# A two-stage Strassen kernel on one Trainium2 core: the low-rank products of two units in one block, a second unit's products brought forward, and another order at the hand-over between the stages

## The chip, the cores and the metric

The kernel runs on one core of one Trainium2 chip. The metric is the device time of one execution in microseconds (us). Everything is in float32. The engines are named as in the profile: PE (TensorE, matmuls), PEld (its weight loads), DVE (VectorE), ACT (ScalarE), POOL (GpSimd) and SP (SyncE, which here only issues DMAs).

## What is computed

`x` is (32, 128, 2048): 32 sequences of 128 tokens. Two layers follow each other, each with a residual:

```python
# layer 0: a dense layer with bias, and a low-rank part chosen by adapter_id (one per sequence)
base  = einsum('bsi,oi->bso', x, weight) + bias          # weight (2048, 2048)
low   = einsum('bsi,bri->bsr', x, lora_a[adapter_id])    # rank 16
delta = einsum('bsr,bor->bso', low, lora_b[adapter_id])
x = x + base + scale[adapter_id] * delta
# layer 1: each sequence has its own (2048, 2048) weight, chosen by another id
x = x + einsum('bij,bkj->bik', x, weight1[adapter_ids])
```

## The kernel before

**Stage 1 (layer 0).** The dense product is made by the Strassen-Winograd scheme on two levels: 7 products in place of 8, at the price of sums and differences of the operands. The outer level is the list `PHASES`: 7 phases, each with the signed quadrants of x and of the weight that are added up to its operands, the partial sum that it reads (`old`), the one that it writes to DRAM (`new`: P1, U2, U3, U4), and, from phase 3 on, the output quadrant that it finishes (`final`). A phase has 8 units (2 groups `g` of sequences x 4 blocks `o` of 256 output channels), so there are 56 units, numbered `n`. Phases 3 to 6 are units 24 to 55.

The inner level is inside a unit: seven calls of `product(k, bank, n, start)`, four accumulating matmuls each (the profile counts two instructions for one float32 matmul), weights 128x128 stationary, 512 columns of x moving. They go in the order 1, 2, 6, 5, 7, 3, 4 into three PSUM banks: a takes products 1, 6, 7, 4, b takes 2, c takes 5 and 3. The sums accumulate in bank a, and ACT copies it out between them (p1 after product 1, u2 after product 6, u3 after product 7, the last quarter of z after product 4); it copies c after product 5. So product 6 adds onto bank a after ACT has copied p1 out of it. Banks a, b and c are double: even and odd units use different ones. DVE adds the banks and copies to the four quarters of `z` (buffer slot 19 or 20, by parity).

DVE also makes the inner operands: `w_sums(n)` (four sums of 128x512, the last three weight operands of `product` come from them), `w_terms` and `a_terms` (the outer sums of 128x2048), and `a_sums` once per four units. `finish(n)`, called at the head of unit n + 1, adds the partial sums and the residual x to z and stores z: to DRAM as a partial sum, or to `x1t`, the input of stage 2.

**The low-rank part.** In phase 1, `lowrank` (L444) makes `low` = scale x (x A), with a row of ones for the bias; `lowrank_out` scales it. `add_low(n, which)` (L491) multiplies it with B and the bias: for each of four 128-column pieces `s` and each of four 32-row groups `q` of the array, one matmul of 32 rows by 128 columns. Phase 3 ("apart", where the unit also has a partial sum to store and so z must stay free of it) sends two groups at a time to the banks d and l and adds them to the residual x. Phases 4 to 6 ("late") send all four at the end of the unit onto b, c, a and d. `load_b` gathers B for the next unit with eight small DMAs on POOL.

**Buffers and queues.** `mem` has 21 slots of 1 MB. `Loads` hands them out in one fixed order of loads: pool "A" (8 slots), "W" (3) and "st" (5, for outer terms, residual x and partial sums). A load is issued on SP when its slot is released, and a load that must wait for a slot holds up all behind it. Each engine runs its own instructions in program order.

**Stage 2 (layer 1).** Sixteen pairs of sequences, 8 steps each, one level of the same scheme: 56 instructions of 128x512 per step (L682), two sequences side by side in 64 columns each. `sums_w1(n)` (L216) adds the identity for the residual to the weight's diagonal blocks and makes the weight sums, all but one, which the function that it returns makes later (`fourth`). `sums_x1` (L248) makes the sums of x1; `load_w1` and `load_x1` load 4 MB and 1 MB. At the end of unit 55 `second_loads` and `second_sums` start this stage: they reuse slots of stage 1, among them slot 19 (z of unit 54) for the x1 sums. The last step has its own order and stores each output quarter as soon as it is ready.

Of the kernel before, what the change touches and what calls it, by code (L numbers as in the profile page):

```python
# [72 lines left out]
def cond_resid_kernel(  # L73
# [103 lines left out]
    def add(dst, a, b):  # L177
        nc.vector.tensor_tensor(dst, a, b, ALU.add)  # L178
# [83 lines left out]
    with tc.tile_pool(name="c0", bufs=1) as c0, tc.tile_pool(  # L262
# [12 lines left out]


        loads = Loads(
            {"A": range(8), "W": (13, 11, 12), "st": (17, 15, 16, 14, 18)}
        )

        def view(slot, *shape):
# [40 lines left out]
                    ),  # L322
                )

        def add_end(n):
            i, g, o = units[n]
            _, _, old, new, final = PHASES[i]

            def load_x(slot):
                r, c, _ = final  # L330
                for t in range(2):
                    nc.sync.dma_start(
                        out=view(slot, 2, 2, NF)[:, t],
                        in_=xq[r, g, t, c, o // 2, :, ts(o % 2, 2)],
                    )

            if final:
                loads.add(("x", n), "st", load_x)
            for k in (old, final[2] if final else None):
                if k:  # L340
                    loads.add(
                        (k, n), "st",
                        lambda slot, k=k: nc.sync.dma_start(out=mem[:, slot], in_=part[k, g, o]),
                    )
# [8 lines left out]
                    )  # L353

        add_w(0)
        for q in range(4):
            add_a(0, q)
        add_w(1)
        for n in range(len(units)):
            if n // 4 + 1 < 2 * len(PHASES):  # L360
                add_a(n // 4 + 1, n % 4)
            if n + 2 < len(units):
                add_w(n + 2)
            add_end(n)
# [123 lines left out]
                    start=(start and i == 0), stop=(i == 3), skip_group_check=True,  # L488
                )

        def add_low(n, which):  # L491

            i, g, o = units[n]
            r = PHASES[i][4][0]
            for s in range(4):
                for q, dst, start in which:
                    nc.tensor.matmul(  # L497
                        dst[:, ts(s, S)], lhsT=b_sels[n][ts(q, RT), s], rhs=low[r, g][ts(q, RT), s],
                        start=start, stop=True, skip_group_check=True,
                    )  # L500

        def zq(z, t, j):

            return z.rearrange("p (t s j m) -> p t s j m", t=2, s=4, j=2)[:, t, :, j]

        def by_seq(psum_bank):
            return psum_bank.rearrange("p (s m) -> p s m", s=4)

        def finish(n):

            i, g, o = units[n]
            _, _, old, new, final = PHASES[i]
            z = mem[:, 19 + n % 2]
            if new:
                w = z
                if old:
                    prev = mem[:, loads.slot((old, n))]
                    w = prev if final else z
                    add(w, prev, z)
                nc.gpsimd.dma_start(out=part[new, g, o], in_=w)  # L520
                if old:
                    loads.done((old, n))
            if final:
                r, c, k = final
                xs = view(loads.slot(("x", n)), 2, 2, 4, S)
                for t in range(2):
                    dst = z.rearrange("p (t s j m) -> p t j s m", t=2, s=4, j=2)[:, t]
                    add(dst, dst, xs[:, t])
                loads.done(("x", n))
                add(z, z, mem[:, loads.slot((k, n))])  # L530
                loads.done((k, n))
                for t in range(2):
                    nc.gpsimd.dma_start(  # L533
                        out=x1t[4 * r + 2 * g + t][:, :, 8 * c + 2 * o : 8 * c + 2 * o + 2].rearrange(
                            "s p j m -> p s (j m)"
                        ),
                        in_=view(19 + n % 2, 2, 4, 2 * S)[:, t],
                    )

        def second_loads():  # L540
            assert n == len(units) - 1 and 19 + n % 2 == 20
# [5 lines left out]
            load_x1(0, 0)  # L547
            load_w1(1)

        def second_sums(step):  # L550
            if step == 5:
                sums_x1(0, 0)
                state["fourth"] = sums_w1(0)
            else:
                state["fourth"]()

        state = {}
        acts, wts, b_sels = {}, {}, {}
        w_terms(0)
        wts[0] = w_sums(0)  # L560
        for _ in a_sums(0):
            pass
        w_terms(1)

        for n, (i, g, o) in enumerate(units):
            _, _, old, new, final = PHASES[i]
            a, b, c = (x[n % 2] for x in (bank_a, bank_b, bank_c))
            z = mem[:, 19 + n % 2]
            group = n // 4
            more = group + 1 < 2 * len(PHASES)  # L570
            lowering = more and (group + 1) // 2 == LOW
            apart = bool(new and final)
            late = final and not apart
            p1, u2, p5, u3 = (
                evp.tile([P, NF], F32, tag=k, name=k) for k in ("p1", "u2", "p5", "u3")
            )
            if n + 1 < len(units) and PHASES[units[n + 1][0]][4]:
                b_sels[n + 1] = load_b(n + 1)
            if n:
                finish(n - 1)  # L580
            if n == 2:
                make_scale()
            if n == len(units) - 2:
                load_w1(0)
            if n + 1 < len(units):
                wts[n + 1] = w_sums(n + 1)
            else:
                second_loads()
            sums = a_sums(group + 1) if more and o == 3 else iter(())

            product(1, a, n, True)
            nc.scalar.copy(p1, a)
            product(2, b, n, True)
            if lowering:
                lowrank(group + 1, o)
                loads.done(("a", group + 1, o))
            if more:
                a_terms(group + 1, o)
            if n + 2 < len(units):
                w_terms(n + 2)  # L600
            if lowering and o % 2 == 1:
                lowrank_out(group + 1, o // 2)
            if not late:
                add(zq(z, 0, 0), by_seq(b), by_seq(p1))
            product(6, a, n, False)
            nc.scalar.copy(u2, a)  # L606
            next(sums, None)
            product(5, c, n, True)
            nc.scalar.copy(p5, c)
            if n + 1 == len(units):  # L610
                second_sums(5)
            next(sums, None)
            if apart:
                add_low(n, [(0, bank_d, True), (1, bank_l, True)])
            product(7, a, n, False)
            nc.scalar.copy(u3, a)  # L616
            if apart:
                xs = view(loads.slot(("x", n)), 2, 2, NF)
                add(xs[:, 0, 0], bank_d, xs[:, 0, 0])
                add(xs[:, 0, 1], bank_l, xs[:, 0, 1])  # L620
            add(zq(z, 1, 1), by_seq(u3), by_seq(p5))
            next(sums, None)
            product(3, c, n, False)
            if apart:
                add_low(n, [(2, bank_d, True), (3, bank_l, True)])
            if not late:
                add(zq(z, 0, 1), by_seq(c), by_seq(u2))
            product(4, a, n, False)
            if apart:
                add(xs[:, 1, 0], bank_d, xs[:, 1, 0])  # L630
                add(xs[:, 1, 1], bank_l, xs[:, 1, 1])
            next(sums, None)
            if late:
                add_low(n, [(0, b, False), (1, c, False), (2, a, False), (3, bank_d, True)])
                add(zq(z, 0, 0), by_seq(b), by_seq(p1))
                add(zq(z, 0, 1), by_seq(c), by_seq(u2))
                add(zq(z, 1, 1), by_seq(bank_d), zq(z, 1, 1))
            nc.scalar.copy(zq(z, 1, 0), by_seq(a))  # L638
            loads.done(("W", n, 0))
            if o == 3:  # L640
                for q in range(4):
                    loads.done(("A", group, q, 0))
            if n + 1 == len(units):
                second_sums(4)
        finish(len(units) - 1)


    with tc.tile_pool(name="c1", bufs=1) as c1:
# [6 lines left out]
        for n in range(last + 1):  # L655
# [13 lines left out]
            elif n % 8 == 6 and pair + 1 < len(pairs):  # L669
                sums_x1(pair + 1, 0)  # L670

            def store(engine, h, c):

                cols = out.rearrange("b t (c m n) -> b t c m n", c=2, m=2)[:, ts(h, M), :, n2]
                for j, b in enumerate(pairs[pair]):
                    engine.dma_start(out=cols[b][:, c], in_=res[ts(j, M), h, c])

            for k in (1, 6, 7, 5, 2, 3, 4) if n == last else (1, 7, 2, 3, 5, 6, 4):
                dst = bank[:, banks[k]]
# [9 lines left out]
                if n == last:  # L689
# [98 lines left out]
```

## Time and profile before

| | us |
|---|---|
| median of 3 runs (lowest, highest) | 2994.54 (2992.4, 2995.85) |
| the profiled execution | 2994.32 |
| its span in the profile | 2992.7 |
| PE busy | 2976.9 |
| DVE busy | 2337.7 |
| ACT busy | 184.2 |
| POOL busy | 239.8 |

The span runs from the first to the last recorded instruction or transfer, and the profiled execution's own time is 1.6 us longer. A line of a group reads: source line, engine, operation, output<-input, shapes, count | busy us, mean ns | idle us of the engine before them and what ended it. Lines of the chain read: start us, length us, what. Stage 1 ends and stage 2 begins near 1443 us.

### The profile page before, as it was taken

The page shows a single profiled execution, that of the slowest core. Times are in us where ns is not written, and L with a number is a line of the kernel's source. Part 1 is how long each engine was busy: PE and PEld are TensorE (multiplying, and loading weights), DVE is VectorE, ACT ScalarE, POOL GpSimd, SP SyncE. Part 2 cuts the span into 40 slices and gives each one's busy share as a digit, 9 for nine tenths or more (in the row PEclk, how much of TensorE's full clock was granted, in tenths as well). Part 3 has the DMA queues.
Part 4 walks back from the last instruction along what each step waited for, and adds up shares of the span by engine and source line. Part 5 has one row for each costly group of instructions (what it writes and reads, how often), then busy time and mean ns, then how long its engine had stood idle before and what let it go on. Part 6 is the DMA issues. An engine that isn't in the chain of part 4 may idle for free.

```text
span 2992.7 us, 32904 instructions
## 1 busy us (share of the span) xinstructions
PE 2976.9 (99%) x12384; PEld 1178.5 (39%) x12384; DVE 2337.7 (78%) x1690; ACT 184.2 (6%) x313; POOL 239.8 (8%) x427
## 2 busy tenths in 40 slices
PE   9999999999999999999999999999999999999999
PEld 4445444444444444444333333333333333333333
DVE  3367755467655669773899999999999999999997
ACT  1111111111111111111000000000000000000000
POOL 1111000012222222221000000000000000000000
PEclk9999999999999999999999999999999999999999
DMA  5679966789866889985999999999999999999996
GB/s 225 239 307 360 343 255 253 266 316 353 311 246 225 305 341 392 393 311 207 367 394 390 390 387 404 388 395 390 402 390 394 393 385 404 385 398 385 407 387 226
DMA packets 186015, 1025.61 MB, mean 343 GB/s; under 512 B 23809, under 2 KB 23809, under 8 KB 79617
## 3 DMA queue, kind: packets, MB, share of 16 engines
q1 hardware_dynamic: 142432, 906.55, 76.5%
q0 software_dynamic: 25248, 83.92, 7.4%
q10 hardware_dynamic: 18176, 33.04, 3.5%
q8 instruction: 98, 1.61, 0.2%
q14 instruction: 61, 0.49, 0.0%
HBM read 922.76 MB, written 100.66 MB: 342 GB/s over the span
## 4 chain that ended last, share of the span: by engine, by line
PE 98%; DMA 1%; DVE 1%; SPq 0%; issue 0%; DVEq 0%
PE bank L682 51%; PE bank L486 44%; PE bank L497 1%; PE bank L453 1%; DMA mem<-in_w1q_dram 1%; DMA mem<-in_xq_dram 0%; DVE mem L181 0%; DVE mem L178 0%; SPq L211 0%; SPq L320 0%; SPq L303 0%; SPq L298 0%; DVE res L178 0%; SPq L243 0%; DVEq L178 0%
## 5 line engine op out<-in xcount | busy, mean ns | idle before, releaser
L181 DVE TENSOR_TENSOR mem<-mem 128x2048 f32<-128x2048 f32 (+1 forms) x733 | 1482.9, 2052 | 30.4 <-PE bank L486 6.3
L682 PE MATMUL bank<-mem 128*64 128x512 f32 x5120 | 1122.6, 593 | 4.4 <-DVE mem L181 2.4
L486 PE MATMUL bank<-mem 128*128 128x512 f32 x1792 | 792.5, 595 | 3.4 <-DMA mem<-in_xq_dram 3.4
L682 PEld LDWEIGHTS bank<-mem 128*64 128x64 f32 x5120 | 367.6, 137 | 737.0 <-issue 689.5
L486 PE MATMUL bank<-mem,tset 128*128 128x512 f32 x1344 | 597.6, 594 | 1.7 <-DVE mem L181 1.5
L486 PEld LDWEIGHTS bank<-mem 128*128 128x128 f32 x1792 | 338.3, 190 | 421.6 <-issue 417.1
L682 PE MATMUL bank<-mem,s 128*64 128x512 f32 x2048 | 461.2, 592 | 0.0
L178 DVE TENSOR_TENSOR mem<-mem 128x2048 f32<-128x2048 f32 (+2 forms) x193 | 338.7, 1769 | 124.9 <-ACT mem L638 56.9
L486 PEld LDWEIGHTS bank<-mem,tset 128*128 128x128 f32 x1344 | 253.7, 190 | 319.7 <-issue 315.7
L682 PEld LDWEIGHTS bank<-mem,s 128*64 128x64 f32 x2048 | 147.1, 137 | 292.4 <-issue 292.1
L178 DVE TENSOR_TENSOR mem<-u,p 128x512 f32<-128x512 f32 x56 | 38.7, 690 | 208.4 <-ACT u L616 208.4
L478 POOL DMA_DIRECT2D b_sel<-in_bt_dram x256 | 135.2, 528 | 580.7 <-PE bank L497 473.3
L178 DVE TENSOR_TENSOR mem<-bank,p 128x512 f32<-128x512 f32 x56 | 38.5, 687 | 126.1 <-PE bank L497 109.4
L688 ACT COPY pv<-bank 128x512 f32<-128x512 f32 x32 | 18.8, 586 | 1515.7 <-PE bank L682 1088.3
L178 DVE TENSOR_TENSOR pv<-bank,pv 128x512 f32<-128x512 f32 x64 | 44.3, 692 | 75.0 <-PE bank L682 74.0
L181 DVE TENSOR_TENSOR tset<-mem,tset 128x512 f32<-128x512 f32 x112 | 77.1, 689 | 8.9 <-PE bank L486 4.1
L178 DVE TENSOR_TENSOR mem<-mem,ident 128x1024 f32<-128x1024 f32 x64 | 78.0, 1219 | 0.0
L178 DVE TENSOR_TENSOR mem<-bank,u 128x512 f32<-128x512 f32 x56 | 38.4, 686 | 45.6 <-PE bank L486 45.6
L606 ACT COPY u<-bank 128x512 f32<-128x512 f32 x56 | 32.8, 586 | 391.8 <-PE bank L486 391.8
L638 ACT COPY mem<-bank 128x512 f32<-128x512 f32 x56 | 32.8, 586 | 387.0 <-PE bank L486 203.3
L533 POOL DMA_DIRECT2D x1t<-mem x64 | 49.2, 773 | 84.0 <-DVE mem L178 79.2
L497 PEld LDWEIGHTS bank<-low,b_sel 32*128 32x128 f32 x1024 | 39.1, 186 | 30.3 <-issue 27.3
(38 smaller groups left out, 519.2 us busy)
## 6 DMA issues: line engine op xcount, KB each, us to landing
mem<-in_w1q_dram SPq DMA_DIRECT2D x512, 1024.0 KB, 10.2
mem<-in_xq_dram SPq DMA_DIRECT2D x119, 1024.0 KB, 12.6
mem<-in_w0q_dram SPq DMA_DIRECT2D x111, 1024.0 KB, 6.9
mem<-U SPq DMA_DIRECT2D x40, 1024.0 KB, 9.0
mem<-in_xq_dram SPq DMA_DIRECT2D x66, 512.0 KB, 7.2
x1t<-mem POOLq DMA_DIRECT2D x64, 512.0 KB, 8.0
mem<-x1t SPq DMA_DIRECT2D x64, 512.0 KB, 9.1
out_dram<-res ACTq DMA_DIRECT2D x124, 256.0 KB, 6.0
```

The lines of the kernel that those rows point to most:

```text
L178: nc.vector.tensor_tensor(dst, a, b, ALU.add)
L181: nc.vector.tensor_tensor(dst, a, b, ALU.subtract)
L453: nc.tensor.matmul(banks_r[r][ts(s, RT), :S], lhsT=a_sel[:, r, s, 4 * k + i, :], rhs=piece[:, i, s, :], start=(h == 0 and seen[r] == 0 and ...
L478: nc.gpsimd.dma_start(out=b_sel[ts(t, 2 * RT), s], in_=bt[ds(m, 1), c, o].rearrange("o j r m -> (o j r) m"),)
L486: nc.tensor.matmul(dst, lhsT=wts[n][k][:, i, :], rhs=acts[n // 4][k][:, i, :], start=(start and i == 0), stop=(i == 3), skip_group_check=True,
L497: nc.tensor.matmul(dst[:, ts(s, S)], lhsT=b_sels[n][ts(q, RT), s], rhs=low[r, g][ts(q, RT), s], start=start, stop=True, skip_group_check=True,
L533: nc.gpsimd.dma_start(out=x1t[4 * r + 2 * g + t][:, :, 8 * c + 2 * o : 8 * c + 2 * o + 2].rearrange("s p j m -> p s (j m)"), in_=view(19 + ...
L606: nc.scalar.copy(u2, a)
L638: nc.scalar.copy(zq(z, 1, 0), by_seq(a))
L682: nc.tensor.matmul(dst[ts(j, M)], lhsT=xts[pair, k4 // 2][k][:, j, k4 % 2 * 2 + i], rhs=w1s[n][k][:, j, i], start=(k4 == 0 and i == 0), st ...
L688: nc.scalar.copy(pv[:, 0], dst)
```

## The change

In phase 3, `add_low(n)` runs once, at the head of the unit, for all four row groups, into the banks b, c, d and l, and DVE adds all four to x (`low_to_x`) there. In phases 4 to 6, an even unit ends with its own `add_low` and directly behind it that of the odd unit n + 1; for the odd one group 0 stays in its bank b (product 2 then adds to it, and now comes ahead of product 1) and the other three are added to its x. x of such a unit is loaded one unit earlier (`early`, `add_x`), and two slots of the pool "st" are swapped. At the start, the weights of unit 1 are loaded ahead of the last two quarters of x, its sums are made ahead of the activation sums, and its products 1 and 2 come between products 2 and 6 of unit 0. The last unit adds x to the partial sum first (`rest`), adds that to z by quarters, makes the first w1 sums ahead of the z addition behind product 7, and stores each half of z as it is ready, without `finish(55)`. The last output store uses SP's queue for one of its two DMAs.

```diff
-            {"A": range(8), "W": (13, 11, 12), "st": (17, 15, 16, 14, 18)}
+            {"A": range(8), "W": (13, 11, 12), "st": (17, 16, 15, 14, 18)}
...
+        def early(n):
+            return n < len(units) and PHASES[units[n][0]][4] and (
+                PHASES[units[n][0]][3] or n % 2 == 1
+            )
...
-            if final:
-                loads.add(("x", n), "st", load_x)
+            if early(n + 1):
+                add_x(n + 1)
+            if final and not early(n):
+                add_x(n)
...
-        for q in range(4):
+        for q in range(2):
             add_a(0, q)
         add_w(1)
+        for q in range(2, 4):
+            add_a(0, q)
...
-        def add_low(n, which):
+        def add_low(n, dsts, starts):
             for s in range(4):
-                for q, dst, start in which:
+                for q, (dst, start) in enumerate(zip(dsts, starts)):
                     nc.tensor.matmul(
                         dst[:, ts(s, S)], lhsT=b_sels[n][ts(q, RT), s], rhs=low[r, g][ts(q, RT), s],
-                        start=start, stop=True, skip_group_check=True,
+                        start=(start and s == 0), stop=(s == 3), skip_group_check=True,
                     )
+        def low_to_x(n, q, src):
+            xs = view(loads.slot(("x", n)), 4, NF)[:, q]
+            add(xs, src, xs)
...
         wts[0] = w_sums(0)
+        w_terms(1)
+        wts[1] = w_sums(1)
         for _ in a_sums(0):
             pass
-        w_terms(1)
...
-            late = final and not apart
+            late = final and not early(n)
+            ahead = early(n) and not apart
...
+            if apart:
+                low_banks = b, c, bank_d, bank_l
+                add_low(n, low_banks, (True,) * 4)
+                for q in range(4):
+                    low_to_x(n, q, low_banks[q])
             if n:
                 finish(n - 1)
...
-            product(1, a, n, True)
-            nc.scalar.copy(p1, a)
-            product(2, b, n, True)
+            if ahead:
+                product(2, b, n, False)
+            if n != 1:
+                product(1, a, n, True)
+                nc.scalar.copy(p1, a)
+                if not ahead:
+                    product(2, b, n, True)
+            if n == 0:
+                p1_next = c0.tile([P, NF], F32, tag="p1_next", name="p1_next")
+                product(1, bank_a[1], 1, True)
+                nc.scalar.copy(p1_next, bank_a[1])
+                product(2, bank_b[1], 1, True)
...
+            if ends:
+                rest = mem[:, loads.slot(("U4", n))]
+                for t in range(2):
+                    dst = rest.rearrange("p (t s j m) -> p t j s m", t=2, s=4, j=2)[:, t]
+                    add(dst, dst, view(loads.slot(("x", n)), 2, 2, 4, S)[:, t])
+                loads.done(("x", n))
             if not late:
                 add(zq(z, 0, 0), by_seq(b), by_seq(p1))
+            if ends:
+                add(zq(z, 0, 0), zq(z, 0, 0), zq(rest, 0, 0))
             product(6, a, n, False)
...
-            if n + 1 == len(units):
-                second_sums(5)
+            if ends:
+                fourth = sums_w1(0)
...
             add(zq(z, 1, 1), by_seq(u3), by_seq(p5))
+            if ends:
+                add(zq(z, 1, 1), zq(z, 1, 1), zq(rest, 1, 1))
+                sums_x1(0, 0)
...
             if not late:
                 add(zq(z, 0, 1), by_seq(c), by_seq(u2))
+            if ends:
+                add(zq(z, 0, 1), zq(z, 0, 1), zq(rest, 0, 1))
+                store_x1(n, 0)
             product(4, a, n, False)
...
             if late:
-                add_low(n, [(0, b, False), (1, c, False), (2, a, False), (3, bank_d, True)])
+                add_low(n, (b, c, a, bank_d), (False, False, False, True))
+                b1, c1, a1 = (x[1 - n % 2] for x in (bank_b, bank_c, bank_a))
+                add_low(n + 1, (b1, c1, a1, bank_l), (True,) * 4)
+                low_to_x(n + 1, 2, a1)
                 add(zq(z, 0, 0), by_seq(b), by_seq(p1))
                 add(zq(z, 0, 1), by_seq(c), by_seq(u2))
                 add(zq(z, 1, 1), by_seq(bank_d), zq(z, 1, 1))
-            nc.scalar.copy(zq(z, 1, 0), by_seq(a))
+                low_to_x(n + 1, 1, c1)
+                low_to_x(n + 1, 3, bank_l)
+            if ends:
+                add(zq(z, 1, 0), by_seq(a), zq(rest, 1, 0))
+                store_x1(n, 1)
+                loads.done(("U4", n))
+                fourth()
+            else:
+                nc.scalar.copy(zq(z, 1, 0), by_seq(a))
...
-            if n + 1 == len(units):
-                second_sums(4)
-        finish(len(units) - 1)
...
-                        store(nc.scalar, 1, 0)
+                        store(nc.scalar, 1, 0, nc.sync)
```

More of the change, by code (lines that the diff above doesn't have):

```diff
@@ L323, in add_a, with add_x @@
                 )
-        def add_end(n):
+        def early(n):
+            return n < len(units) and PHASES[units[n][0]][4] and (
+                PHASES[units[n][0]][3] or n % 2 == 1
+            )
+        def add_x(n):
             i, g, o = units[n]
-            _, _, old, new, final = PHASES[i]
             def load_x(slot):
-                r, c, _ = final
+                r, c, _ = PHASES[i][4]
                 for t in range(2):
@@ L335, in load_x, with add_end @@
                     )
-            if final:
-                loads.add(("x", n), "st", load_x)
+            loads.add(("x", n), "st", load_x)
+        def add_end(n):
+            i, g, o = units[n]
+            _, _, old, new, final = PHASES[i]
+            if early(n + 1):
+                add_x(n + 1)
+            if final and not early(n):
+                add_x(n)
             for k in (old, final[2] if final else None):
@@ L504, in zq, with store_x1 @@
             return z.rearrange("p (t s j m) -> p t s j m", t=2, s=4, j=2)[:, t, :, j]
+        def low_to_x(n, q, src):
+            xs = view(loads.slot(("x", n)), 4, NF)[:, q]
+            add(xs, src, xs)
         def by_seq(psum_bank):
             return psum_bank.rearrange("p (s m) -> p s m", s=4)
+        def store_x1(n, t):
+            i, g, o = units[n]
+            r, c, _ = PHASES[i][4]
+            nc.gpsimd.dma_start(
+                out=x1t[4 * r + 2 * g + t][:, :, 8 * c + 2 * o : 8 * c + 2 * o + 2].rearrange(
+                    "s p j m -> p s (j m)"
+                ),
+                in_=view(19 + n % 2, 2, 4, 2 * S)[:, t],
+            )
         def finish(n):
@@ L532, in finish @@
                 for t in range(2):
[L533 to L538, printed above, removed]
+                    store_x1(n, t)
         def second_loads():
@@ L548, in second_loads @@
             load_w1(1)
[L550 to L557, printed above, removed]
         acts, wts, b_sels = {}, {}, {}
@@ L576, in cond_resid_kernel @@
             )
+            if n == 1:
+                p1 = p1_next
             if n + 1 < len(units) and PHASES[units[n + 1][0]][4]:
                 b_sels[n + 1] = load_b(n + 1)
+            if apart:
[3 more added lines that the diff above has]
+                    low_to_x(n, q, low_banks[q])
             if n:
@@ L584, in cond_resid_kernel @@
                 load_w1(0)
-            if n + 1 < len(units):
+            if 0 < n < len(units) - 1:
                 wts[n + 1] = w_sums(n + 1)
-            else:
+            elif n:
                 second_loads()
             sums = a_sums(group + 1) if more and o == 3 else iter(())
-            product(1, a, n, True)
-            nc.scalar.copy(p1, a)
-            product(2, b, n, True)
+            if ahead:
[10 more added lines that the diff above has]
+                product(2, bank_b[1], 1, True)
             if lowering:
@@ L602, in cond_resid_kernel @@
                 lowrank_out(group + 1, o // 2)
+            ends = n + 1 == len(units)
+            if ends:
[4 more added lines that the diff above has]
+                loads.done(("x", n))
             if not late:
                 add(zq(z, 0, 0), by_seq(b), by_seq(p1))
+            if ends:
+                add(zq(z, 0, 0), zq(z, 0, 0), zq(rest, 0, 0))
             product(6, a, n, False)
@@ L609, in cond_resid_kernel @@
             nc.scalar.copy(p5, c)
-            if n + 1 == len(units):
-                second_sums(5)
+            if ends:
+                fourth = sums_w1(0)
             next(sums, None)
-            if apart:
-                add_low(n, [(0, bank_d, True), (1, bank_l, True)])
             product(7, a, n, False)
             nc.scalar.copy(u3, a)
[L617 to L620, printed above, removed]
             add(zq(z, 1, 1), by_seq(u3), by_seq(p5))
+            if ends:
+                add(zq(z, 1, 1), zq(z, 1, 1), zq(rest, 1, 1))
+                sums_x1(0, 0)
             next(sums, None)
             product(3, c, n, False)
-            if apart:
-                add_low(n, [(2, bank_d, True), (3, bank_l, True)])
             if not late:
                 add(zq(z, 0, 1), by_seq(c), by_seq(u2))
+            if ends:
+                add(zq(z, 0, 1), zq(z, 0, 1), zq(rest, 0, 1))
+                store_x1(n, 0)
             product(4, a, n, False)
-            if apart:
-                add(xs[:, 1, 0], bank_d, xs[:, 1, 0])
-                add(xs[:, 1, 1], bank_l, xs[:, 1, 1])
             next(sums, None)
             if late:
-                add_low(n, [(0, b, False), (1, c, False), (2, a, False), (3, bank_d, True)])
+                add_low(n, (b, c, a, bank_d), (False, False, False, True))
+                b1, c1, a1 = (x[1 - n % 2] for x in (bank_b, bank_c, bank_a))
+                add_low(n + 1, (b1, c1, a1, bank_l), (True,) * 4)
+                low_to_x(n + 1, 2, a1)
                 add(zq(z, 0, 0), by_seq(b), by_seq(p1))
@@ L670, in cond_resid_kernel, with store @@
                 sums_x1(pair + 1, 0)
-            def store(engine, h, c):
+            def store(engine, h, c, other=None):
                 cols = out.rearrange("b t (c m n) -> b t c m n", c=2, m=2)[:, ts(h, M), :, n2]
                 for j, b in enumerate(pairs[pair]):
-                    engine.dma_start(out=cols[b][:, c], in_=res[ts(j, M), h, c])
+                    (other if j and other else engine).dma_start(out=cols[b][:, c], in_=res[ts(j, M), h, c])
             for k in (1, 6, 7, 5, 2, 3, 4) if n == last else (1, 7, 2, 3, 5, 6, 4):
```

## The prediction

> **What bounds the kernel now.** I read the page first (busy shares, chain), then the groups kept apart by shape, the chain of waits in order of time, and the timeline of single engines where that chain leaves PE.
>
> ```profile
> span 2992.7 us, 32904 instructions
> PE 2976.9 (99%) x12384; PEld 1178.5 (39%) x12384; DVE 2337.7 (78%) x1690; ACT 184.2 (6%) x313; POOL 239.8 (8%) x427
> PE 98%; DMA 1%; DVE 1%; SPq 0%; issue 0%; DVEq 0%
> ```
>
> PE is the bound: what doesn't shorten PE's row of work, or close a hole in it, is worth nothing. The chain (start, length, what) shows what a low-rank block costs inside that row. In phase 3 ("apart") a unit has two blocks of 16 instructions, in phases 4 to 6 ("late") one of 32:
>
> ```profile
> 285.25 3.63 PE bank L453 x128
> 288.88 24.23 PE bank L486 x56
> ...
> 316.74 319.50 PE bank L486 x744
> 636.24 1.09 PE bank L497 x16
> 637.33 7.06 PE bank L486 x16
> 644.39 1.09 PE bank L497 x16
> 645.48 17.36 PE bank L486 x40
> ...
> 859.40 1.10 PE bank L497 x32
> 860.51 24.23 PE bank L486 x56
> ```
>
> A block's line says 1.1 us for 16 instructions as for 32, but the stretch of 56 behind it is longer than 56 of the 744 without a block: 56 x 319.50/744 = 24.05 us. So a late unit's block costs 24.23 + 1.10 - 24.05 = 1.28 us, an apart unit's two (7.06 + 1.09 + 17.36 + 1.09 - 24.05)/2 = 1.28 each, and `lowrank` (L453) 3.81. The two holes in PE's row are at the start and where stage 1 hands over to stage 2 (PE's timeline; the bracket is idle time and what ended it):
>
> ```profile
> 6.84 3.60 PE L486 MATMUL bank<-mem 128*128 128x512 f32 x8
> 13.85 5.37 PE L486 MATMUL bank<-mem 128*128 128x512 f32 x8 [3.41 <-DMA mem<-in_xq_dram]
> 20.36 2.36 PE L486 MATMUL bank<-mem,tset 128*128 128x512 f32 x4 [1.13 <-DVE mem L181]
> 22.92 1.12 PE L486 MATMUL bank<-mem,tset 128*128 128x512 f32 x2 [0.20 <-DVE mem L181]
> 24.25 4.56 PE L486 MATMUL bank<-mem,tset 128*128 128x512 f32 x10 [0.20 <-DVE mem L181]
> ...
> 1443.12 1.94 PE L682 MATMUL bank<-mem 128*64 128x512 f32 x8
> 1446.12 10.52 PE L682 MATMUL bank<-mem 128*64 128x512 f32 x48 [1.06 <-DVE mem L181]
> 1458.66 3.28 PE L682 MATMUL bank<-mem 128*64 128x512 f32 x8 [2.01 <-DVE mem L178]
> 1463.31 12.24 PE L682 MATMUL bank<-mem 128*64 128x512 f32 x56 [1.37 <-DVE mem L181]
> ```
>
> From 24.25 to 1445 and from 1463 to the end PE doesn't stop. A product (8 instructions) takes 24.05/7 = 3.43 us.
>
> **1. Apart units, 24 to 31.** Two blocks become one of four row groups at the head of the unit: 8 x (2 x 1.28 - 1.28) = **-10.2 us**. The four additions to x move from after p7 and p4 to DVE's head of the unit, ahead of `finish(n-1)` and `w_sums(n+1)`. Only p2 (bank b) and p5 (bank c) wait for them; p1 (3.43 us) covers, as the first addition ends some 0.8 us after the block. Where DVE is late the cover shrinks: unit 27 also makes group 7's sums, and its DVE work end to end (4 x 0.60 + 7.0 + 2.6 + 2 x 2.2 + 3 x 0.6 + 4 x 2.2) ends at about 28.3 us, the first addition of unit 28 at 28.9, p2 wants it at 29.7. 0.8 us of slack; a late transfer makes a stall of it.
>
> **2. Late pairs, units 32 to 55.** Two blocks of 32 become one of 64. What of 1.28 us is fixed? `lowrank` puts 32 instructions on each of four groups of the array and costs 3.81 us, a low block 8 on each and costs 1.28: (3.81 - 1.28)/24 = 0.105 us per instruction, 0.44 fixed. A pair: 16 x 0.105 + 0.44 = 2.12, against 2.56. Ends: 1.68 (nothing fixed), 2.56 (nothing shared). 12 x 0.44 = **-5.3 us**.
> A rule speaks against this: the Trainium skill ("TensorE: Matmul & The Clock Gate", Part 3, and its LDWEIGHTS section) has a weight load overlap running matmuls only where the row group differs, and gives about columns/1.2 ns for it, 107 ns here. Then 16 turns of 0.21 us make a pair 3.4 us and more, and the edit costs 12 x 0.9 = 11 us. But by the same rule the old block needs 8 x 0.21 = 1.7 us, and the rows give 1.28 with its fixed part. The row decides.
>
> **3. The odd unit's new order.** In odd late units ("ahead") p2 now goes first, since bank b holds a low part already, and then p1, copy of p1, p6. p6 adds onto p1's bank and waits for ScalarE's copy. Before, p2 stood between and hid it:
>
> ```profile
> 860.44 7.13 PE L486 MATMUL bank<-mem 128*128 128x512 f32 x16
> 864.22 0.59 ACT L592 COPY p<-bank 128x512 f32<-128x512 f32 x1 [3.02 <-PE bank L486]
> ...
> 871.08 0.59 ACT L606 COPY u<-bank 128x512 f32<-128x512 f32 x1 [6.28 <-PE bank L486]
> ```
>
> In the changed PE order p6 follows p1 at once, with a wait on ScalarE. Queued behind it is all of PE's unit. Price: p1's last instruction streams until 860.54 + 3.43 = 863.97 (0.11 for the first weight load); the copy starts 0.25 later and takes 0.59; a released PE starts within 0.04 (24.21 to 24.25 in the start) and loads weights for 0.11. Together 0.99 us; ends 0.63 (copy and release alone) and 1.25. 12 units: **+11.9 us**. This is twice what the pairing gains. The wait of p1 for `low_to_x` (bank a) is covered by p2: it ends 0.8 us after the pair, p2 takes 3.43.
> Does the 1 us hole cost clock too? The granted clock (column PEclk; the column after it is DMA's share):
>
> ```profile
> 15.35:18.75 3.40, 3.40 (x6) 1.17 (x4) 0.00 (x0) 0.00 (x0) 0.00 (x0) 0.51 1.02 431
> 1459.20:1462.60 3.40, 2.74 (x8) 0.44 (x4) 3.37 (x2) 0.00 (x0) 0.06 (x1) 0.51 0.99 387
> 1440.00:1459.00 19.00, 15.92 (x95) 5.53 (x95) 18.79 (x15) 0.59 (x1) 1.24 (x2) 1.00 1.01 410
> ```
>
> Half clock followed the holes of 3.41 and of 2.01 us, and not the one of 1.06. The skill (same page, Part 1) has the half rate follow at least one idle window of about 3.4 us; by that the 2.01 us hole should have cost nothing. The row corrects it, downwards; 1 us stays on the safe side, but no longer by far. By rule and row: 0. If a 1 us hole tripped it, 1.7 us each, +20.
>
> **4. Start.** W of unit 1 is loaded ahead of the last two x quarters, `w_sums(1)` ahead of the activation sums, and p1, p2 of unit 1 run before p6 of unit 0. The 3.41 us hole and its half clock stay. The x quarters landed 2.48 us apart in the trace (13.7, 16.2, 18.7): W1 takes the place at 16.2, so the sums come 2.5 us later, s2's first chunk at 20.2 + 2.5 = 22.7, its last at 24.2 + 2.5 = 26.7. PE: p2 to 19.1, p1 and p2 of unit 1 to 26.0, p6 then finds each chunk ready (the last is wanted at 28.6). At 24.25 PE has done 28 instructions instead of 22: 6 x 0.43 = **-2.6 us** (ends -1 and -3).
>
> **5. Handover.** From 1443.12 to 1463.31 PE runs 64 instructions, worth 64 x 0.2145 = 13.7 us: 6.5 us lost, 1.7 of them to the half clock. Why: DVE stood 10.9 us in `sums_x1(0,0)` until the store of unit 54 released slot 19 (1435.25), with the sums, unit 55's four additions and `finish(55)` queued behind. Now rest = U4 + x is added early, the w1 sums stand before that wait, `finish(55)` is gone, and the x1 slot (18 instead of 16) is free earlier, so that `load_x1(0,0)` no longer waits for DVE on SP's queue. Unit 55's DVE work end to end from the pair: additions 3.7, `finish(54)` to 8.3, rest 10.7, z 11.9, w1 sums 19.9, z 21.1, x1 sums 23.6 (the stores, issued near 8.4, took 13.5 us before, so 22), z 25.9, fourth 28.2; stage 2 starts at 25.1, wants s3 at 26.8, t4 at 35, b12 of step 1 at 39 (ready 34). Nothing is late: **-6.2 us** (ends -3, -6.5). Next late: DVE, which is 96 to 100% busy in stage 2, with 4 us of slack at step 2.
>
> **6. End.** The last output half is issued on SP beside ScalarE's queue. Issues there are 0.51 us apart: **-0.5 us**.
>
> **Costed at nothing.** The extra DVE additions (10 per pair instead of 8, 1.2 us): DVE is busy 365 of 569 us in 848 to 1417. Tight only in units 43 to 46, where four-term sums keep DVE at 111 of 125 us and DMA at a share of 1.01. There x(n+1), 1 MB, now passes A, W and partial sums on SP's queue, and takes one of five slots a unit earlier: everything behind it lands about 2.5 us later. Unit 45's last addition ended at 1191.4; about 4 us later it still meets p6 of unit 46 with some 1.8 us left. For this and unit 28 I add **+0.7 us** (ends 0 and 8). `load_b` on POOL keeps its place; its reader comes half a unit earlier in phase 3, over 20 us after landing.
>
> **Sum**, against the profiled execution, 2994.32 us (0.2 below the median of the runs): -10.2 - 5.3 + 11.9 - 2.6 - 6.2 - 0.5 + 0.7 = -12.2, so 2982.1, given as 2982.0.
>
> **Rivals.**
> *The copy is hidden after all*: for it, ScalarE is 6% busy; against it, the order of PE. Then 2982.1 - 11.9 = 2970.2.
> *DVE and DMA take the gain*: the tight spots stall (8 us), or the handover gives 3 us only, or both: 2985 to 2993. For it, landings of 12 to 19 us after issue in units 45 to 47; against it, PE never waited there.
> *Slower*: the hole of each odd unit trips the clock, 1.7 us more in each. With 7 of 12 the gain is gone, with 11 the kernel is 6 us slower, with 12 it takes 2982.1 + 20.4 = 3002.5. For it, 2.01 us sufficed; against it, 1.06 us did not.
> *The change doesn't group*: four row groups would run one by one. Excluded: 32 instructions cost no more than 16.
>
> **How the numbers follow.** My sum with its bounds, 2978 to 2987: 0.72. Copy hidden: 0.06. DVE and DMA take the gain: 0.17. Slower: 0.05. A measurement of this kernel tells 0.2%, 6 us, from no change; the line is at 2988.5. Below it lie the first two cases and 0.03 of the third, 0.81; within it 0.15; 0.04 above (the slower case with its clock tripped nearly throughout; its rest is within). Range 2976 to 2990: it takes in the ends of the pair and the copy and half of the third case.
>
> **What would show it.** In the profile after: blocks of `add_low` costing 1.28 us for 32 instructions and 2.12 for 64, by unit lengths; twelve waits of PE or PEld for ScalarE's p1 copy, about 1 us each; PE without a stop from 13.85; no wait at the handover; granted clock 1.00 from unit 32 to 55. I am wrong if PE waits on DVE or DMA in units 25 to 31 or 44 to 47, or if the copies cost nothing or clock.

## The result and the profile after

| | before | after |
|---|---|---|
| median of 15 runs each, us | 2994.06 (2992.34 to 2996.49) | 2988.12 (2986.55 to 2991.45) |
| the profiled execution, us | 2994.32 | 2988.26 |
| its span, us | 2992.7 | 2986.6 |

The ratio of after to before is 0.998, 95% interval 0.9973 to 0.9986: 5.9 us faster where 12 were forecast. The new time lies in the range that was given (2976 to 2990), near its upper end. The two profiled executions lie within 0.3 us of their medians, so they can be compared step by step. The kernel before was measured again beside each set of experiments, and its medians ran from 2994.06 to 2995.36 us: differences of about 1 us between sets say nothing.

The page of after, span, busy shares and chain:

```profile
span 2986.6 us, 32858 instructions
PE 2964.9 (99%) x12384; PEld 1171.9 (39%) x12384; DVE 2351.8 (79%) x1717; ACT 183.6 (6%) x312; POOL 239.0 (8%) x427
PE 74%; DVE 1%; DMA 0%; ACT 0%; issue 0%; ACTq 0%; DVEq 0%
```

PE is still the bound, but where the chain was 98% PE it is 74%, and it names ACT. (The shares don't fill the span: the chain begins near 724 us, behind a wait that it can't follow further back.) In order of time it shows what has changed inside PE's row (start, length, what; `product` is now L500, `add_low` L511, stage 2 L728):

```profile
727.87 23.85 PE bank L500 x48
751.72 1.10 PE bank L511 x32
752.82 24.23 PE bank L500 x56
777.05 1.10 PE bank L511 x32
...
851.75 2.00 PE bank L511 x64
...
860.90 0.59 ACT p L619
...
861.54 41.47 PE bank L500 x96
903.00 2.00 PE bank L511 x64
```

An apart unit takes 777.05 - 751.72 = 25.33 us now, against 26.60. Two late units take 903.00 - 851.75 = 51.25 us, against 2 x 25.33 = 50.67. Between p1 and p6 of the odd unit stands ACT's copy of p1. And at 727.87 PE starts again, in the middle of unit 28. PE's timeline, with idle time in brackets, gives the size of that stop and what ended it (DVE), and shows the start and the hand-over:

```profile
7.71 3.60 PE L500 MATMUL bank<-mem 128*128 128x512 f32 x8
12.85 10.54 PE L500 MATMUL bank<-mem 128*128 128x512 f32 x24 [1.53 <-DMA mem<-in_xq_dram]
...
718.37 1.17 PE L511 MATMUL bank<-low,b_sel 32*128 32x128 f32 x32
719.48 3.70 PE L500 MATMUL bank<-mem 128*128 128x512 f32 x8
727.87 6.68 PE L500 MATMUL bank<-mem 128*128 128x512 f32 x8 [4.69 <-DVE mem L178]
...
751.65 1.17 PE L511 MATMUL bank<-low,b_sel 32*128 32x128 f32 x32
...
1443.50 25.97 PE L728 MATMUL bank<-mem 128*64 128x512 f32 x120
```

The eight instructions behind the stop took 6.68 us instead of 3.6: PE was granted half of its clock, called a half clock below. The windows around it and at the start (PEclk is the last column but two):

```profile
15.35:18.75 3.40, 3.40 (x9) 1.52 (x8) 2.46 (x4) 0.00 (x0) 0.00 (x0) 1.00 1.02 429
714.00:740.00 26.00, 21.31 (x73) 9.30 (x72) 25.67 (x21) 1.76 (x3) 2.73 (x5) 0.87 0.78 296
```

So unit 28 took 751.65 - 718.37 = 33.3 us, 8.0 more than its neighbours: 4.7 idle, 6.68 - 3.60 = 3.1 half clock, the rest release and weight load. The start lost 1.53 us, with full clock in the window where before it was 0.51. At the hand-over PE doesn't stop at all. What held DVE there before was this wait of the x1 sums for the store of unit 54:

```profile
1435.25 0.69 DVE L178 TENSOR_TENSOR mem<-mem 128x512 f32<-128x512 f32 x1 [10.89 <-DMA x1t<-mem]
```

In after the same sums begin near 1439.6 us with no wait in front of them.

**Where the time went**, by four marks in PE's row of both traces (us). The heads of units 24 and 32 are reckoned from the blocks next to them, from what their instructions take without a stop.

| stretch | before | after | moved |
|---|---|---|---|
| to the head of unit 24 (start) | 622.5 | 617.1 | -5.4 |
| units 24 to 31 (apart) | 212.9 | 210.6 | -2.2 |
| units 32 to 55 (late) | 607.8 | 615.8 | +8.0 |
| first to last group of stage 2 (hand-over) | 1542.9 | 1536.5 | -6.4 |
| behind it, to the end of the span | 6.7 | 6.6 | 0 |

**Why DVE was late in unit 28.** DVE's timeline at the second W term of unit 29, before, where it did not wait:

```profile
714.65 2.29 DVE L181 TENSOR_TENSOR mem<-mem 128x2048 f32<-128x2048 f32 x1
```

and after, over units 27 and 28:

```profile
706.08 2.29 DVE L178 TENSOR_TENSOR mem<-mem 128x2048 f32<-128x2048 f32 x1
714.12 2.29 DVE L181 TENSOR_TENSOR mem<-mem 128x2048 f32<-128x2048 f32 x1 [5.75 <-DMA mem<-in_w0q_dram]
...
727.13 2.48 DVE L178 TENSOR_TENSOR mem<-bank,mem 128x512 f32<-128x512 f32 x4
```

At 708.37 DVE was ready for the second W term of unit 29 and stood 5.75 us for its transfer, with the sums of group 7 and unit 28's additions to x (the line `mem<-bank,mem`) queued behind. p2 wanted the first of these at 722.9 and got it at 727.8. The transfer was late because its issue was late. SP's queue with the W transfers of unit 29 and its wait in this stretch, first before, then after:

```profile
697.64 0.80 SPq L298 DMA_DIRECT2D mem<-in_w0q_dram  x2
...
SPq L332 <- DMA U<-mem: 15.4, 1, 15.4
```

```profile
690.25 17.36 SPq L298 DMA_DIRECT2D mem<-in_w0q_dram  x2
...
SPq L298 <- DMA U<-mem: 16.6, 1, 16.6
```

Before, the two W transfers took 0.80 us to issue, after 17.36, most of it the wait in front of the second. The queue stands some 16 us for a slot in both kernels, until the store of a partial sum has landed. Before, the load that stood there was x (L332), whose reader came later in the unit and did not wait in unit 27. Now x of the next unit goes ahead in the order of loads and holds a slot longer, and the one that stands there is W (L298). No run here puts x back behind W in phase 3: that the early x is why W stands there is read from the order of loads and these waits, not tested by an edit.

### The profile page after: what moved, and what is told of

Its sections match the earlier page's. It is cut to its first block, busy times and chain, and to the rows that moved or that the text cites. A ratio compares the mean times of both kernels' runs of the same rounds, so it can differ in the third digit from the quotient of the medians.

```text
span 2986.6 us, 32858 instructions
## 1 busy us (share of the span) xinstructions
PE 2964.9 (99%) x12384; PEld 1171.9 (39%) x12384; DVE 2351.8 (79%) x1717; ACT 183.6 (6%) x312; POOL 239.0 (8%) x427
## 4 chain that ended last, share of the span: by engine, by line
PE 74%; DVE 1%; DMA 0%; ACT 0%; issue 0%; ACTq 0%; DVEq 0%
PE bank L728 52%; PE bank L500 22%; PE bank L511 1%; DMA mem<-in_w0q_dram 0%; DVE mem L178 0%; ACT p L619 0%; DVE mem L181 0%; DVE tset L181 0%; DVE res L178 0%; ACTq L619 0%; DVEq L178 0%; DVEq L181 0%
## 5 line engine op out<-in xcount | busy, mean ns | idle before, releaser
L728 PE MATMUL bank<-mem 128*64 128x512 f32 x5120 | 1120.6, 592 | 0.0
L500 PE MATMUL bank<-mem 128*128 128x512 f32 x1792 | 792.7, 595 | 6.2 <-DVE mem L178 4.7
L728 PEld LDWEIGHTS bank<-mem 128*64 128x64 f32 x5120 | 367.7, 137 | 731.1 <-issue 695.2
L500 PE MATMUL bank<-mem,tset 128*128 128x512 f32 x1344 | 597.1, 594 | 9.2 <-ACT p L619 9.2
L500 PEld LDWEIGHTS bank<-mem 128*128 128x128 f32 x1792 | 339.6, 191 | 429.5 <-issue 421.4
L728 PE MATMUL bank<-mem,s 128*64 128x512 f32 x2048 | 461.2, 592 | 0.0
L500 PEld LDWEIGHTS bank<-mem,tset 128*128 128x128 f32 x1344 | 253.5, 190 | 333.3 <-issue 309.2
L728 PEld LDWEIGHTS bank<-mem,s 128*64 128x64 f32 x2048 | 147.1, 137 | 292.4 <-issue 291.5
L178 DVE TENSOR_TENSOR mem<-bank,mem 128x512 f32<-128x512 f32 x81 | 51.4, 684 | 104.4 <-PE bank L511 104.4
L619 ACT COPY p<-bank 128x512 f32<-128x512 f32 x55 | 32.2, 586 | 231.1 <-PE bank L500 224.8
## 6 DMA issues: line engine op xcount, KB each, us to landing
mem<-in_w1q_dram SPq DMA_DIRECT2D x512, 1024.0 KB, 10.2
```

What stands on the lines that cost most here:

```text
L500: nc.tensor.matmul(dst, lhsT=wts[n][k][:, i, :], rhs=acts[n // 4][k][:, i, :], start=(start and i == 0), stop=(i == 3), skip_group_check=True,
L728: nc.tensor.matmul(dst[ts(j, M)], lhsT=xts[pair, k4 // 2][k][:, j, k4 % 2 * 2 + i], rhs=w1s[n][k][:, j, i], start=(k4 == 0 and i == 0), st ...
```

## The experiments

All are compared with after, 2988.12 us, unless said otherwise.

**e1: another bank.** p2 of an apart unit no longer waits for DVE.

```diff
-                low_banks = b, c, bank_d, bank_l
+                low_banks = bank_b[1 - n % 2], c, bank_d, bank_l
```

> Edit to the changed kernel: in units 24 to 31 the first quarter of the low part goes to bank b of the other parity instead of the unit's own, so that p2 no longer waits for DVE's addition to x. My theory: the lost 8.0 us of unit 28 are 4.96 us in which p2 waited for that addition and 3.1 us of half clock behind it, and both go: 2980.1 us, unit 28 takes 25.3 us like its neighbours. Rival, 'DVE is too late altogether': DVE is still 5 us behind, and p5 (bank c) or unit 29 stalls instead: 2983 to 2988. Rival, 'the wait is an artefact of the profiled execution': no change, 2988.

Measured: 2981.31 us (2979.87 to 2983.09), ratio to before 0.9956 (0.9943 to 0.997). PE's timeline of e1 in unit 28:

```profile
719.21 1.17 PE L511 MATMUL bank<-low,b_sel 32*128 32x128 f32 x32
720.31 7.13 PE L500 MATMUL bank<-mem 128*128 128x512 f32 x16
```

and DVE's, at the same W term:

```profile
716.26 2.29 DVE L181 TENSOR_TENSOR mem<-mem 128x2048 f32<-128x2048 f32 x1 [7.23 <-DMA mem<-in_w0q_dram]
```

W is as late as in after, and DVE waits even longer, 7.23 us. But p1 and p2 run through, the run's granted clock is 1.000 where after had 0.999, and no later reader stalls: 6.8 of the 8.0 us come back by the medians.

**e2: the late transfer's reader moved.** Unit 27 alone; the banks stay as in after.

```diff
-            if n + 2 < len(units):
+            if n + 2 < len(units) and n != 27:
                 w_terms(n + 2)
...
             product(4, a, n, False)
             next(sums, None)
+            if n == 27:
+                w_terms(n + 2)
```

> Edit to the changed kernel: in unit 27 alone the addition of the second W term for unit 29, for whose transfer DVE stood 5.75 us, moves from ahead of the activation sums to behind them. The banks stay as they are. My theory: DVE's 0.8 us of slack was right and the late transfer was the cause; without it the first addition to x of unit 28 ends near 722, p2 wants it at 722.9, no stall: 2980.1 us. Rival, 'DVE has too much to do in unit 27 even without the wait': a stall of 1 to 4 us stays and above 2 us the clock dips too, 2982 to 2986.

Measured: 2980.43 us (2980.27 to 2982.13), ratio 0.9954 (0.9941 to 0.9968). DVE's timeline of e2:

```profile
721.71 2.48 DVE L178 TENSOR_TENSOR mem<-bank,mem 128x512 f32<-128x512 f32 x4
```

The first addition to x ends near 722.3, just ahead of p2. Two edits that have nothing in common, one on the bank and one on the wait for W, take away the same 7 to 8 us: the stall needs both the late W and the bank. DVE's own work in unit 27 is not too much.

**e3: p2 cut in two around p1**, so that half of p2 hides the copy (`product` now takes the steps that it runs).

```diff
             if ahead:
-                product(2, b, n, False)
+                product(2, b, n, False, (0, 1))
             if n != 1:
                 product(1, a, n, True)
                 nc.scalar.copy(p1, a)
+                if ahead:
+                    product(2, b, n, False, (2, 3))
```

> Edit to the changed kernel: in odd late units p2 is cut in two, two matmuls of it before p1 and two between p1 and p6, so that 1.7 us of p2 stand between p1 and p6 and hide ScalarE's copy, and 1.7 us stand before p1. My theory: each of the 12 holes costs about 1.0 us (0.71 us idle, the rest release and weight load), and goes: 12 x 0.97 = 11.6, 2976.5 us, the stretch from pair to pair falls from 51.25 to 50.3. Rival, 'the 3.15 us above the products are the pair's own': the holes go from the chain but the stretch stays near 51: at most -3 us, 2985. Rival, 'p1 stalls now, as the addition to x of bank a is not ready after 1.7 us': 2980 and above.

Measured: 2977.98 us (2976.21 to 2980.22), ratio 0.9946 (0.9932 to 0.996). The chain of e3:

```profile
902.69 2.00 PE bank L511 x64
904.69 48.27 PE bank L500 x112
```

The hole is gone and the stretch from pair to pair is 50.26 us: the hole cost 51.25 - 50.26 = 0.99 us, and the pair itself 50.26 - 2 x 24.05 = 2.16. By the medians 10.1 us came back, not 11.6: 0.9 us of the rest are at units 45 and 46, which lost 1.8 us here instead of 0.9. The rest is within what the medians of two sets scatter.

**e4: e1 and e3 together.**

> Edit to the changed kernel: the other bank of e1 and the split p2 of e3 together. If the two losses are independent, their gains add: 2988.1 - 8.0 - 11.6 = 2968.5 us. If the time that unit 28 gives back brings DVE or the loads behind in the units after it, less: 2970 to 2976.

Measured: 2971.79 us (2969.93 to 2973.87), ratio 0.9924 (0.991 to 0.9937): less than the sum, by 3.3 us. The timelines of DVE, ACT and PE in e4 over units 45 and 46:

```profile
1170.80 2.29 DVE L181 TENSOR_TENSOR mem<-mem 128x2048 f32<-128x2048 f32 x1 [5.14 <-DMA mem<-in_w0q_dram]
...
1180.15 0.58 ACT L619 COPY p<-bank 128x512 f32<-128x512 f32 x1 [7.86 <-DVE mem L178]
...
1180.78 8.72 PE L500 MATMUL bank<-mem,tset 128*128 128x512 f32 x16 [2.25 <-ACT p L619]
```

DVE waits for W terms, with unit 45's addition of bank b and p1 behind that wait (it runs at 1179.37). ACT can't overwrite p1 for unit 46 until this addition has read it, and PE waits for ACT. This is the other tight spot that the prediction named; the faster kernel meets it harder, 54.36 us for the two units instead of 50.26.

**e8: that addition ahead of the wait.** Edit to e4:

```diff
+            if ahead and not n + 1 == len(units):
+                add(zq(z, 0, 0), by_seq(b), by_seq(p1))
             if more:
                 a_terms(group + 1, o)
             if n + 2 < len(units):
                 w_terms(n + 2)
...
-            if not late:
+            if not late and (ends or not ahead):
                 add(zq(z, 0, 0), by_seq(b), by_seq(p1))
```

> Edit to e4: in odd late units (the last apart) DVE's first addition to z (bank b + p1) moves from behind the W terms of two units later to ahead of the A and W terms. In e4 the stretch of units 45 and 46 took 54.36 us instead of 50.26: DVE waited for a W transfer with that addition behind it, ScalarE's p1 copy of unit 46 waited for the addition (7.86 us), and PE for the copy (2.25 us, then a half clock). My theory: with the addition ahead of the wait the stretch falls to 50.3: 2971.8 - 4.1 = 2967.7 us. Rival, 'the transfers are late in these units, whatever waits for them': the next reader stalls (w sums of unit 47, or p6 of it): 2970 to 2973.

Measured: 2969.68 us (2967.94 to 2971.12), ratio 0.9913 (0.9899 to 0.9926), the fastest here, 26 us below before. Its chain over units 45 and 46:

```profile
1148.92 2.00 PE bank L511 x64
1150.91 48.26 PE bank L500 x112
```

50.26 us, no stall. DVE still waits 5.0 us for W there, with nothing urgent behind it. The median is 2.0 us above the forecast; before was 1.3 us slower in this set than beside after. The profiled run, the slowest of the five, is 3.5 us late by unit 24 already: its start had a hole of 4.03 us and a half clock.

**e5 and e9: the pairs undone.** e5 undoes all of them:

```diff
-                PHASES[units[n][0]][3] or n % 2 == 1
+                PHASES[units[n][0]][3]
...
-                add_low(n + 1, (b1, c1, a1, bank_l), (True,) * 4)
-                low_to_x(n + 1, 2, a1)
...
-                low_to_x(n + 1, 1, c1)
-                low_to_x(n + 1, 3, bank_l)
```

> Edit to the changed kernel: the pairs are undone, every late unit (32 to 55) has its own block of 32 behind p4 and p1 before p2 as in the kernel before; the start, units 24 to 31 and the end stay as changed. My theory: pairs with their hole cost more than they save, 3.15 us a pair against 2 x 1.28, 12 x 0.59 = 7.1, and 0.9 us more are lost at unit 46: 2988.1 - 8.0 = 2980.1 us. Rival, 'the pairing is a gain and unit 28 the only loss': 2988 or slower.

Measured: 2984.97 us (2982.78 to 2986.37). All late units have 25.33 us, but PE stops at the hand-over. PE's and DVE's timelines of e5:

```profile
1441.96 8.80 PE L723 MATMUL bank<-mem 128*64 128x512 f32 x40 [2.61 <-DVE mem L178]
...
1441.21 0.69 DVE L178 TENSOR_TENSOR mem<-bank,p 128x512 f32<-128x512 f32 x1 [9.88 <-DMA x1t<-mem]
```

This stop comes from a fault of e5. Its last unit is a late one again, whose additions to the first half of z now stand behind the store of that half: the store sends out what lay there from an earlier unit plus U4 + x, and the additions then overwrite it. DVE waits 9.88 us for that store before it may do so, and PE waits for the bank that this addition reads. A second stop, of 0.97 us, follows some ten us later, with DVE still behind. So e5's time says nothing of the new end; less these two stops it would be near 2981.4 us (an estimate). e9 avoids the fault and keeps the last pair (the two slots of the pool "st" are back in their old order there):

```diff
-                PHASES[units[n][0]][3] or n % 2 == 1
+                PHASES[units[n][0]][3] or n == len(units) - 1
...
+                if early(n + 1):
                     add_low(n + 1, (b1, c1, a1, bank_l), (True,) * 4)
                     low_to_x(n + 1, 2, a1)
...
+                if early(n + 1):
                     low_to_x(n + 1, 1, c1)
                     low_to_x(n + 1, 3, bank_l)
```

> Mended form of e5, where the last unit's quarters lost U4 + x: the pairs are undone in units 32 to 53, and kept for 54 and 55, on which the new end relies; two slot numbers are swapped to fit. e5 showed that without the last pair the handover stalls again, 2.6 and 1.0 us. My theory: 11 pairs at 3.15 us become 22 blocks at 1.28: 11 x 0.59 = 6.5, and the 0.9 us of unit 46 come back: 2988.1 - 7.4 = 2980.7 us. Rival, 'the early x is what keeps the units around the handover fed': 2984 or more, with waits of stage 2 as in e5.

Measured: 2981.65 us (2980.74 to 2982.38), ratio to before 0.9955 (0.9941 to 0.9968). So eleven pairs with their holes, and the loss at unit 46, cost 6.5 us net against the old order by the medians (7.4 forecast). Whether the new end would work without the twelfth pair was not measured.

**e6: the start alone**, on the kernel before. The changed lines are those of the start in the diff above.

> Edit to the kernel before: the changed start alone (W of unit 1 loaded and summed early, p1 and p2 of unit 1 before p6 of unit 0). My forecast gave it 2.6 us with the hole of 3.4 us and its half clock kept; the trace of the changed kernel has a hole of 1.53 us, no half clock and 34.4 instructions done at 24.25 us instead of 22, 5.3 us. Theory of the trace: 2994.1 - 5.3 = 2988.8. Forecast's: 2991.5.

Measured: 2991.37 us (2988.99 to 2992.97, 18 runs) against 2994.91, ratio 0.9987 (0.9979 to 0.9994), -3.5 us: between the two forecasts, and the interval (-6.3 to -1.8 us) holds both. PE's timeline of its profiled run:

```profile
14.55 12.23 PE L488 MATMUL bank<-mem 128*128 128x512 f32 x24 [3.91 <-DMA mem<-in_xq_dram]
```

Here the quarter of x came 1.7 us later than in after, the hole was 3.91 us, and a half clock followed (12.23 us for 24 instructions, 10.54 in after). The profiled runs with this start have holes of 1.53 to 4.03 us, and the half clock in some. By their heads of unit 24, against the one profiled execution of before, the gain of the start scatters from -1.9 to -5.4 us.

**e7 and e10: longer holes.** ACT copies p1 three times (e7) or twice (e10) in the odd late units:

```diff
                 nc.scalar.copy(p1, a)
+                if ahead:
+                    nc.scalar.copy(p1, a)
+                    nc.scalar.copy(p1, a)    # e7 alone
```

> Edit to the changed kernel: ScalarE copies p1 three times instead of once in odd late units, so that the hole before p6 grows from 0.71 us idle to about 1.9 us, with the same work for PE. It asks where the clock gives way, which decides my 'slower' rival. If 1.9 us does not trip the half clock: 12 x 1.2 = +14 us, 3002.5, granted clock 1.00 in units 33 to 55. If it does in all twelve, 1.7 to 3.1 us more each: 3023 to 3040.

Measured: 3020.16 us in one run, between the two cases. PE's timeline of e7 behind the first and the third hole, and the windows that follow on these holes:

```profile
865.46 8.83 PE L500 MATMUL bank<-mem,tset 128*128 128x512 f32 x16 [1.95 <-ACT p L622]
...
973.81 7.13 PE L500 MATMUL bank<-mem,tset 128*128 128x512 f32 x16 [1.95 <-ACT p L622]
```

```profile
866.15:869.55 3.40, 3.40 (x6) 1.36 (x5) 1.77 (x3) 0.00 (x0) 1.55 (x3) 0.50 0.90 298
...
975.40:978.80 3.40, 3.40 (x9) 1.49 (x8) 0.87 (x2) 0.58 (x1) 1.23 (x3) 1.00 0.79 262
```

The same hole of 1.95 us costs the clock at 866 and not at 975. Nine of the twelve are followed by 3.41 us of half clock (1.7 us lost in each), three are not. The nine half clocks start at 866.15, 920.77, 1026.58 us and so on, always whole multiples of 3.413 us apart. On that grid the nine holes lie wholly in one step, the three others are cut by an edge and leave at most 1.85 us in one step.

> Edit to the changed kernel: ScalarE copies p1 twice in odd late units, hole about 1.3 us. In e7 a half clock of 3.41 us followed 9 of 12 holes of 1.9 us, and the clock record of it lies on a grid of 3.41 us; the nine holes lay wholly in one step of the grid, the three others were cut by an edge, with at most 1.85 us in one step. By that, a step needs more than some 1.85 us of idle PE, and a hole of 1.3 us never trips: 12 x 0.6 = +7, 2995.3 us, granted clock 1.00 in units 33 to 55 (but for unit 46). Rival, 'any hole above about 1 us can trip': some of the twelve cost 1.7 us more, 2997 to 3015.

Measured: 2993.52 us in one run. The twelve holes of 1.34 us, some within one step and some cut, cost their length and no clock, and unit 28 had one step of half clock in this run where after had two, 1.6 us less. The window of e10 over the pairs:

```profile
852.00:1420.00 568.00, 553.27 (x1887) 251.12 (x1882) 378.39 (x332) 70.64 (x121) 127.01 (x220) 1.00 0.79 303
```

## Why the prediction was right and wrong

- **Part 1, apart units: right.** 8 x (26.60 - 25.33) = 10.2, as forecast.
- **The tight spots: this step failed.** They were put at +0.7 us for unit 28 and units 43 to 46 together, with ends 0 and 8. They cost 8.0 at unit 28 and 0.9 at unit 46 (52.13 us instead of 51.25). The slack of 0.8 us was right: DVE was late by 5.75 us of waiting, less 0.8 gives 4.95, and PE lost 4.9 before the clock's part (e1 takes away what p2 had to wait for, e2 the wait for W, and the loss goes with either). "A late transfer makes a stall of it" was right as well. The error was in asking for late transfers only in units 43 to 46. The early x passes W on SP's queue in phase 3 too, and the queue's wait for the store of the partial sum, which cost PE nothing in front of x, now stands in front of W (that the early x does this is argued, not tested). Three more us came from the half clock, which the prediction had priced only for its copy holes. The rival "DVE and DMA take the gain" (2985 to 2993) is what happened, by its first branch alone: the tight spots stalled, and the hand-over gave its full gain.
- **Parts 2 and 3, pair and copy hole: right.** 12 x (51.25 - 50.67) = +7.0, forecast +6.6. e3 and e8 separate them: 2.16 us a pair (2.12 forecast, and 3.4 by the estimate from the skill's figure, which was set aside) and 0.99 a hole (0.99 forecast). That 2.12 came so close is in part luck: its fixed share was taken from `lowrank`, whose weights are 128 rows by 32 columns and not 32 by 128. That the holes leave the clock alone was right, and e7 shows where the slower rival begins: with holes of 1.95 us nine of twelve trip it, with 1.34 none (e10).
- **Part 4, start: mis-sized, in the other direction.** -2.6 forecast, -5.4 in the profiled execution. It assumed that the hole of 3.41 us and its half clock stay. They are not fixed: the quarter of x landed 1 us earlier and p1 began 0.9 later in this execution. Over 18 runs the start alone is worth 3.5 us, with an interval of 1.8 to 6.3 (e6). So some of the 5.4 may be luck of the two profiled executions.
- **Part 5, hand-over: right.** -6.4 against -6.2, and the wait that it named is gone. No run takes the edits of this part one by one.
- **Part 6, end: nothing.** The last two stores are issued side by side, the later one 0.5 us nearer to the last addition, but it took 2.9 us from issue to landing instead of 2.4, and the span still ends 4.7 us behind that addition.

The sum with the measured terms: -10.2 + 8.0 + 7.0 + 0.9 - 5.4 - 6.4 = -6.1, and the profiled executions differ by 6.06. Against the forecast of -12.2, the tight spots account for +8.2 us (8.9 instead of 0.7), the start gives 2.8 back, and the other terms add 0.7.

## What to carry to other kernels

When a load is brought forward in a queue that hands out slots in order, look at which load inherits the place where the queue stands, and who waits for that one: a wait of 16 us did no harm in front of x and went with a loss of 8 us in front of W. A slack under 1 us behind an engine that waits for transfers should be priced as gone; putting the urgent reader ahead of the wait, or its result in a bank that nobody wants soon, is a one-line cure (e1, e2, e8). An accumulating product that adds onto a bank being copied out cost 0.99 us here with nothing between, and nothing with half of a neighbouring product, 1.7 us, between.

## What the runs showed of the hardware

The half clock follows idle time counted in fixed steps, not the length of a hole. Over the twelve profiles, from the first product on, every full-clock step of the 3.413 us grid with 1.95 us or more of idle PE was followed by a half clock, and none with 1.92 us or less. A hole of 3.33 us cut into 1.92 and 1.41 (e7's start) cost no clock, one of 1.95 within a step cost 1.7 us. In a step that already ran at half clock, 0.79 and 1.09 us of idle brought a second one (after and e7 at unit 28), and 0.58 and 0.59 did not (e5, e10). The Trainium skill ("TensorE: Matmul & The Clock Gate", Part 1) has a free-running window of 3413 ns, and the grid here agrees. Its advice to leave no PE gaps of more than about 3 us (same page, "Why this matters for your kernels") is too lenient here: in a step at full clock less than 1.9 us of idle time was safe, and for holes from there to some 3.8 us (an estimate, twice 1.92) it mattered where the step's edge fell. With the changed start, a hole of 2.32 us brought a half clock (e3), and holes of 2.93 and 3.18 us did not (e1, e9). The scatter of one kernel's runs may come from this in part, as the start's hole, 1.53 to 4.03 us in these profiles, meets the edge differently in each; no run shows it for one kernel alone.
